# A four-layer graph network on one core: layer 3's seams rearranged (four propagations first, logits inside the late attentions, the check behind the next step's first logits, end flags earlier)

## The chip, the core and the metric

The kernel runs on one core of a Trainium2 chip. A core has five engines with queues of their own: TensorE (PE; its weight loads are shown apart as PEld), VectorE (DVE), ScalarE (ACT), GpSimd (POOL) and SyncE (SP), which here issues most DMAs. They wait for each other by semaphores. The metric is the device time in microseconds (us) of one execution. Times inside an execution are counted from its first instruction.

## The reference, cut to what matters

3327 nodes with 256 features pass through four layers, each of the form `x = x + layer(relu(layernorm(x)))` over the same 3327 x 3327 adjacency. Layers 0 to 2 are products with the adjacency (the second keeps at most 700 entries of a row; the kernel counts a row's entries for this). Layer 3 is the one the change is about:

```python
R = (S + I) / rowsum                       # propagation, S = adj
Z = 0; Xf = Xa = X
for n in range(2):                         # two steps
    q = Xa @ W1.T @ W2.T;  k = Xa @ W3.T
    probs = softmax(q @ k.T)
    A = probs kept up to 0.9 of the row's mass, renormalized   # top-p
    Xf = R @ Xf                            # propagation
    Xa = A @ Xa                            # attention
    Z = Z + Xf @ U1[n].T + Xa @ U2[n].T
h = X + Z;  out = layernorm(h) * g + b
```

The second step's keys come from the first step's attention of all nodes, so all of attention 1 must be done before the first logits of step 2.

## The kernel before, in words

Rows are tiled by 128: T = 26 tiles (the last has 127 rows). All of layer 3 is in `layer_3_in`. PE's order there is written out by hand (`tc.manual_schedule(engines=PE_ALONE)`); the other engines' queues are put in order by the framework from dependencies, program order and priorities, and are then fixed. For one tile m there are these pieces:

- **Propagation** (`propagated_steps`, L1058): 26 blocks, 52 PE instructions, on two adjacency slabs of 832 KB loaded by SP (L1055, three buffers); POOL adds the identity to one block (L1057). The generator yields after each block, and a plan `at = {block: [things to do]}` puts other PE work after a block. Then `PropagationOfFirstStep`: ACT scales the result (`xf`, L1099), SP loads `hT` (L1101); later `turn` (two transposes, L136) and `sums` (8 products, L1111, copied by ACT at L1113).
- **Logits** (`logits_steps`, L912): four chunks into PSUM (two buffers, `ps_row`, shared with node, values and sums), each turned into exponentials by ACT (L931) in a tile `e` (three buffers). `spread` puts two chunks after each of two blocks of a propagation.
- **Search** (`search_steps`): finds for each row the least kept probability. First a threshold from the row's sum (L947 on DVE, L948 to L952 in turns with ACT), then two passes over `e` on ACT (L963, the shortfall; L965, a sign count), then DVE alone: L967 to L1006, among them a 3328-wide pass (L973), maxima (L986, L991), and the masking of `e` (L1002). L1006 ends the search. In the tile loop the two ACT passes and the rest are placed by `passes` after groups 0, 2 and 3 of an attention.
- **Attention** (`Rows.begin`: transposes of the first 8 blocks of the masked `e`, L177, copied by ACT to `eT`, L180; `Rows.finish`: 52 products, L188, with the other transposes between, a yield after each group of four blocks). It needs its own search done. After it `AttentionOfFirstStep`: ACT scales (`xa`, L1069), then `turn`, `node` (key and query of the second step, L241) and `values` (L1082; ACT copies `vs`, L1088, DVE adds `z`, L1089, SP stores it, L1090).

The order before, in the first step: propagations 0, 1, 2 (logits of tiles 0 and 1 inside them), logits 2, then for m = 0 to 25 attention m; up to m = 19 propagation m+3 follows, with the logits of tile m+3, and the turn, node and values of m and `begin(m+1)` put inside (after blocks 0 and 12, and 3, 9, 18, 20). For m = 20 to 25 there is no propagation: logits, turn, node, values and the next transposes simply follow one another. Propagation m's turn and sums stand after groups 1 and 5 of attention m. The search of tile m+2 runs beside attention m.

After attention 25: `failed` (L1024 to L1042, with a matmul that adds up flags over rows, L1034), propagation 23, then `if_failed`: each engine loads a flag into a register and jumps over the repair code (L1241, L1242 in the profile). Behind it the second step begins: key sum and centring of the keys (L887 to L901), logits 0, search 0, propagations 24 and 25 with logits 1 and 2. In the second step every tile has an attention and a propagation, then `finish3`: DVE adds (L1124), normalizes (L1126 to L1131), POOL does three further operations (L1132 to L1134), SP stores to `out` (L1136). At the very end: flags and check of the second step, then a maximum over the row counts (L1416 to L1422) and a second check (L1424) that would run everything again.

Of the kernel before, what the change touches and what calls it, by code (L numbers as in the profile page):

```python
# [45 lines left out]
def kernel(  # L46
# [782 lines left out]
    def layer_3(again, h3, kT0, ksum0, left):  # L829
        tag = "b" if again else "a"  # L830

        only_exp_and_ln()
        with ExitStack() as lctx:
            big, ep, w3, sm3 = (
                lctx.enter_context(tc.tile_pool(name=f"{n}{tag}", bufs=b))
                for n, b in (("big", 1), ("ep", 3), ("w3", 2), ("sm3", 4))
            )
            layer_3_in(tag, big, ep, w3, sm3, h3, kT0, ksum0, left)

    def layer_3_in(tag, big, ep, w3, sm3, h3, kT0, ksum0, left):  # L840
# [53 lines left out]
        def centre(kT, pk, name):  # L894

            mean = sm3.tile([P, 1], F32, tag="kmean", name=f"kmean_{name}{tag}")
            with tc.high_priority():
                nc.vector.tensor_scalar(mean, pk[:, :1], -1.0 / N, None, ALU.mult)
                for r, n in ((0, LOW * P), (DA, N - LOW * P)):
                    k = kT[r : r + DA, :n]  # L900
                    nc.vector.tensor_scalar(k, k, mean[r : r + DA, :], None, ALU.add)  # L901

# [19 lines left out]
        def scores(step, m, kT):  # L922
# [5 lines left out]
            nc.gpsimd.memset(parts[:, len(CHUNKS) :], -1.0)  # L928

            def evict(c, dst, src):  # L930
                nc.scalar.activation(dst, src, AF.Exp, accum_out=parts[:, c : c + 1])  # L931

            return e, parts, logits_steps(kT, qT[:, m * P : (m + 1) * P], e, name, evict)

        def search_steps(step, m, e, parts, st, dens):
# [29 lines left out]
            nc.scalar.activation(junk_a, e, AF.Sign, scale=-1.0, bias=t, accum_out=sign)  # L965
            yield 2
            nc.vector.tensor_scalar(u, sign, 0.5, NP / 2 - AIM, ALU.mult, ALU.add)  # L967
# [147 lines left out]
        def finish3(m, y, acc, name):  # L1115
# [16 lines left out]
            nc.gpsimd.tensor_tensor(z, z, gs, ALU.mult)  # L1132
            nc.gpsimd.tensor_tensor(z, z, bs, ALU.add)
            nc.gpsimd.tensor_tensor(z, z, x3, ALU.add)  # L1134
# [30 lines left out]
        def redone(step, m, kT, name, evict):  # L1165
            e = ep.tile([P, NP], F32, tag="e", name=f"e_{name}")
# [25 lines left out]
        def by_least(step, m, kT, gen, st):  # L1192
# [8 lines left out]
            e = redone(step, m, kT, name, lambda c, dst, src: nc.scalar.activation(dst, src, AF.Exp))  # L1201
# [16 lines left out]
        def general(step, m, kT, gen):  # L1218
# [3 lines left out]
            e = redone(step, m, kT, name, lambda c, dst, src: nc.scalar.copy(dst, src))  # L1222
# [14 lines left out]
        def if_failed(step, flags, st, kT, then):  # L1237
            def inside(level, i, gen):
# [3 lines left out]
                with tc.If(n > 0):  # L1242
                    if level:
                        with tc.tile_pool(name=f"gen{step}", bufs=1) if not gen else nullcontext(gen) as g:
                            for k in range(3):
                                inside(level - 1, 3 * i + k, g)
                    else:
                        e, den, bad = by_least(step, i, kT, gen, st)
                        then(i, e, den, f"t{i}")
                        n_bad = nc.values_load(bad)  # L1250
                        with tc.If(n_bad > 0):
                            then(i, *general(step, i, kT, gen), f"g{i}")
# [5 lines left out]
        EARLY = 3  # L1258
        LATE = 3

        with tc.manual_schedule(engines=PE_ALONE):
# [7 lines left out]
            def find(step, m, st):  # L1269
                return search_steps(step, m, *made[m][:2], st, dens)  # L1270
# [46 lines left out]

            for i in range(EARLY):
                if i == 0:
# [3 lines left out]
                elif i == 1:  # L1323
                    steps = prepare(0, 0, kT0)
                    propagate_first(1, merged({3: [lambda: centre(kT0, mean0(), "0")]}, spread(steps, 9, 19)))
                    run(find(0, 0, st0))
                else:
                    first, second = prepare(0, i - 1, kT0), None
                    propagate_first(i, spread(first))
                    finder = find(0, i - 1, st0)  # L1330
                    run(finder)
            run(prepare(0, EARLY - 1, kT0))
            finder = find(0, EARLY - 1, st0)
            rows = Rows(0, h3)
            rows.begin(0)
            for m in range(T):
                plan = passes(finder)
                if props:
                    p = props.pop(0)
                    plan = merged(plan, {1: [p.turn], 5: [p.sums]})  # L1340
                a = AttentionOfFirstStep(m, rows.finish(m, plan), dens.pop(m), f"{m}")
                after = {3: [a.turn], 9: [a.node], 18: [a.values], 20: [lambda: rows.begin(m + 1)]}
                steps = prepare(0, m + AHEAD, kT0) if m + AHEAD < T else iter(())
                if m + EARLY < T - LATE:
# [127 lines left out]
```

## Time and profile before

| | us |
|---|---|
| median of 3 runs | 2678.3 (2676.7 to 2678.89) |
| profiled execution | 2678.22 |
| its span, first to last instruction | 2676.3 |
| PE busy in the span | 2581.7 |
| first propagation of layer 3 | 957.4 |
| first attention (first step) | 1025.8 |
| attention 19, 20 | 1672.4, 1706.4 |
| attention 24, 25 | 1802.8, 1821.3 |
| end of propagation 23 | 1850.1 |
| first attention (second step) | 1908.9 |
| last product of PE | 2658.9 |

A line of the timeline or of a group reads: start and busy time, engine, line of the kernel, operation, what it writes and reads, how often; in brackets the idle time of the engine before it and what ended it. A window's row gives the stretch, its length, then the busy time and the number of instructions of each engine, the granted PE clock (1.00 is full), the DMA share and GB/s.

### The profile page before, as it was taken

To read this page: it belongs to the slowest core of one execution; us is meant where nothing else is said; L and a number is where in the kernel's file an instruction comes from. 1 tells how busy PE (TensorE), PEld (TensorE's weight loads), DVE (VectorE), ACT (ScalarE), POOL (GpSimd) and SP (SyncE) were. 2 spreads that over 40 slices of the span, in tenths; PEclk is the share of its full clock that TensorE was granted. 3 is DMA by queue.
4 is the path that set the end of the run, shared out by engine and by line. 5 is a ranking of instruction groups with operands and counts; after the bars stand their busy time and mean duration, and the time that the engine had idled before them with its cause. 6 is when DMAs were issued, how large, how long until landed. Compare 5 with 4: busy or idle time off the path is not lost. (4 is left out here: it accounts for less than half of the span.)

```text
span 2676.3 us, 42731 instructions
## 1 busy us (share of the span) xinstructions
PE 2581.7 (96%) x15979; PEld 2219.4 (83%) x15979; DVE 2038.3 (76%) x5488; ACT 1035.3 (39%) x1877; POOL 219.1 (8%) x438
## 2 busy tenths in 40 slices
PE   6999999999999997999999999988999999999997
PEld 6999999999999975777777777766787888788786
DVE  6667788888877748777777776692988888888882
ACT  2110034433011135444444455563454455445441
POOL 2000010000000000000000000000011111111111
PEclk9999999999999998999999999999999999999999
DMA  6555555555666621111111111101122122112211
GB/s 220 145 158 167 168 152 175 172 172 164 187 197 200 190 94 56 60 56 55 54 56 57 58 60 61 50 12 49 62 84 69 64 89 69 64 66 87 69 64 52
DMA packets 141357, 273.42 MB, mean 102 GB/s; under 512 B 15427, under 2 KB 67904, under 8 KB 141120
## 3 DMA queue, kind: packets, MB, share of 16 engines
q1 hardware_dynamic: 115648, 252.49, 29.6%
q10 hardware_dynamic: 25472, 17.92, 2.2%
q8 instruction: 131, 2.15, 0.3%
q14 instruction: 106, 0.87, 0.1%
HBM read 248.20 MB, written 20.45 MB: 100 GB/s over the span
## 5 line engine op out<-in xcount | busy, mean ns | idle before, releaser
L188 PE MATMUL a<-h3a,eT_a 128*128 128x256 f32 x1352 | 325.7, 382 | 8.7 <-ACT eT_a L180 8.5
L1058 PE MATMUL f<-h3a,slab3a 128*128 128x256 f32 x1352 | 323.6, 383 | 0.2 <-issue 0.2
L188 PE MATMUL a<-vs,eT_a 128*128 128x256 f32 x1352 | 322.5, 383 | 0.4 <-ACT eT_a L180 0.2
L1058 PE MATMUL f<-fsa,slab3a 128*128 128x256 f32 x1352 | 312.5, 382 | 0.0
L1058 PEld LDWEIGHTS f<-h3a,slab3a 128*128 128x128 f32 x1352 | 247.7, 190 | 60.4 <-issue 28.1
L1058 PEld LDWEIGHTS f<-fsa,slab3a 128*128 128x128 f32 x1352 | 249.8, 189 | 52.8 <-issue 16.7
L986 DVE MAX8 cand_a<-w 128x8 f32<-128x128 f32 x1352 | 283.3, 280 | 6.7
L188 PEld LDWEIGHTS a<-h3a,eT_a 128*128 128x128 f32 x1352 | 246.1, 190 | 45.0 <-ACT eT_a L180 15.7
L188 PEld LDWEIGHTS a<-vs,eT_a 128*128 128x128 f32 x1352 | 246.3, 190 | 37.5 <-ACT eT_a L180 6.3
L180 ACT COPY eT_a<-pt_a 128x512 f32<-128x512 f32 (+1 forms) x364 | 195.7, 553 | 205.4 <-PE pt_a L177 201.9
L519 PE MATMUL acc_a<-tsa,s_a 128*128 128x128 f32 (+1 forms) x2028 | 268.4, 275 | 0.7 <-DVE tsa L331 0.7
L931 ACT ACTIVATE e_a<-pl_a 128x1024 f32<-128x1024 f32 x208 | 177.9, 860 | 205.8 <-PE pl_a L912 205.7
L519 PE MATMUL acc_a<-tsa,a_a 128*128 128x128 f32 x2028 | 251.2, 275 | 1.8 <-DVE tsa L334 1.8
L519 PE MATMUL acc_a<-rhs,a_a 128*128 128x128 f32 (+1 forms) x2028 | 250.5, 276 | 0.0
L519 PEld LDWEIGHTS acc_a<-tsa,s_a 128*128 128x128 f32 x2028 | 247.4, 192 | 1.2 <-DVE tsa L331 1.0
L519 PEld LDWEIGHTS acc_a<-tsa,a_a 128*128 128x128 f32 x2028 | 239.7, 192 | 3.1 <-DVE tsa L334 2.2
L519 PEld LDWEIGHTS acc_a<-rhs,a_a 128*128 128x128 f32 x2028 | 238.4, 192 | 1.9 <-ACT rhs L411 0.4
L982 DVE SCALAR_TENSOR_TENSOR w<-e_a,t_a 128x896 f32<-128x896 f32 x208 | 225.0, 1082 | 5.2
L177 PE MATMUL pt_a<-ident,e_a 128*128 128x128 f32 x1352 | 200.5, 274 | 13.2 <-DVE e_a L1002 10.9
L177 PEld LDWEIGHTS pt_a<-ident,e_a 128*128 128x128 f32 x1352 | 165.9, 141 | 54.2 <-ACT eT_a L180 11.5
L967 DVE TENSOR_SCALAR u_a<-sign_a 128x1 f32<-128x1 f32 x52 | 8.0, 154 | 245.8 <-ACT junk_a L965 245.8
L973 DVE SCALAR_TENSOR_TENSOR w<-e_a,t_a 128x3328 uint8<-128x3328 f32 x52 | 191.6, 3684 | 3.6
(202 smaller groups left out, 3498.6 us busy)
## 6 DMA issues: line engine op xcount, KB each, us to landing
slab3a<-in_adj_t_dram SPq DMA_DIRECT2D x104, 832.0 KB, 5.9
a_a<-in_adj_t_dram SPq DMA_DIRECT2D x312, 256.0 KB, 3.3
a_a<-in_adj_t_dram SPq DMA_DIRECT2D x156, 320.0 KB, 3.4
x_dram<-x_a ACTq DMA_DIRECT2D x39, 256.0 KB, 2.7
x_a<-x_dram SPq DMA_DIRECT2D x26, 256.0 KB, 3.1
hT_dram<-xT_a ACTq DMA_DIRECT2D x26, 128.0 KB, 3.7
hT<-hT_dram SPq DMA_DIRECT2D x26, 128.0 KB, 2.0
z_dram<-z SPq DMA_DIRECT2D x26, 128.0 KB, 1.7
```

The source lines that it names most:

```text
L177: nc.tensor.transpose(pt[:, j, :], e[:, k * P : (k + 1) * P], ident)
L180: last_turned.append(nc.scalar.copy(eT[:, : len(blocks), :], pt[:, : len(blocks), :]))
L188: nc.tensor.matmul(acc[:, :width], ready[g][:, j, :], rhs[:, k, :], start=(k == 0), stop=(k == T - 1))
L519: nc.tensor.matmul(self.acc[:, g, at : at + wide], quads[n][:, k - CUTS[c][0], :], t, start=(k == 0 and n in (1, 4)), stop=(k == H - 1 and ...
L931: nc.scalar.activation(dst, src, AF.Exp, accum_out=parts[:, c : c + 1])
L967: nc.vector.tensor_scalar(u, sign, 0.5, NP / 2 - AIM, ALU.mult, ALU.add)
L973: nc.vector.scalar_tensor_tensor(junk, e, t, e, ALU.is_lt, ALU.mult, accum_out=got)
L982: nc.vector.scalar_tensor_tensor(w[:, : (b - a) * P], eg, t, eg, ALU.is_lt, ALU.mult, accum_out=below[:, g : g + 1])
L986: nc.vector.max(cand[:, 8 * k : 8 * k + 8], w[:, (k - a) * P : (k - a + 1) * P])
L1058: nc.tensor.matmul(acc[:, :D], slab[g][:, j, :], xf[:, k, :], start=(n == 0), stop=(n == T - 1))
```

## The change

Four propagations instead of three stand first; the first three's turn and sums go inside the following propagations, the fourth's comes after it. From m = 1 on, attention m carries the turn and sums of propagation m+3. For the first tile of each step the sign pass is done on DVE (`alone`) instead of ACT. Attentions without a propagation behind them (m = 19 to 23) carry the logits of tile m+3 after groups 4 and 6; the next tile's transposes follow at once, then the turn, and node and values go after groups 0 and 2 of the next attention. Propagation 23 stands between attentions 24 and 25. Propagation 24 follows attention 25 and carries its turn, node and values, the flags, the key sum, the centring and the logits of the second step's first tile. Only then comes the check. Behind it: search 0, propagation 25 with the logits of tiles 1 and 2. At the end the flags of the second step are computed inside the last propagation, the last tile's three POOL operations go to DVE, and the maximum over the counts with its flag is computed after layer 2, its register loaded before the check of the second step. The repair code (`by_least`, `general`, `redo_first`) gets a scratch tile and redoes the first logits and a key's centring; it is jumped over in these runs.

```diff
+        def exp_of_logits(step, m, kT, e, parts, name=""):
...
             nc.scalar.activation(junk_a, e, AF.Relu, scale=-1.0, bias=t, accum_out=short)
             yield 1
-            nc.scalar.activation(junk_a, e, AF.Sign, scale=-1.0, bias=t, accum_out=sign)
+            if alone:
+                nc.vector.tensor_scalar(junk, e, t, None, ALU.is_lt, ALU.add, accum_out=sign)
+            else:
+                nc.scalar.activation(junk_a, e, AF.Sign, scale=-1.0, bias=t, accum_out=sign)
             yield 2
...
-            nc.gpsimd.tensor_tensor(z, z, gs, ALU.mult)
-            nc.gpsimd.tensor_tensor(z, z, bs, ALU.add)
-            nc.gpsimd.tensor_tensor(z, z, x3, ALU.add)
+            engine = nc.vector if m == T - 1 else nc.gpsimd
+            engine.tensor_tensor(z, z, gs, ALU.mult)
+            engine.tensor_tensor(z, z, bs, ALU.add)
+            engine.tensor_tensor(z, z, x3, ALU.add)
...
-        EARLY = 3
+        EARLY = 4
...
+                return search_steps(step, m, *made[m][:2], st, dens, m == 0)
...
             for i in range(EARLY):
+                plan = {}
+                if props:
+                    p = props.pop(0)
+                    plan = {5: [p.turn], 16: [p.sums]}
...
-                    first, second = prepare(0, i - 1, kT0), None
-                    propagate_first(i, spread(first))
+                    propagate_first(i, merged(spread(prepare(0, i - 1, kT0)), plan))
                     finder = find(0, i - 1, st0)
-                    run(finder)
-            run(prepare(0, EARLY - 1, kT0))
-            finder = find(0, EARLY - 1, st0)
+                    if i + 1 < EARLY:
+                        run(finder)
+            p = props.pop(0)
+            p.turn()
+            p.sums()
             rows = Rows(0, h3)
             rows.begin(0)
+            left_over = {}
             for m in range(T):
-                plan = passes(finder)
+                plan = merged(passes(finder), left_over)
                 if props:
                     p = props.pop(0)
                     plan = merged(plan, {1: [p.turn], 5: [p.sums]})
+                interleaved = m + EARLY < T - LATE
...
+                    plan = merged(plan, {4: [begin_logits], 6: [lambda: next(steps)]})
                 a = AttentionOfFirstStep(m, rows.finish(m, plan), dens.pop(m), f"{m}")
...
-                else:
-                    run(steps)
-                    for k in sorted(after):
-                        after[k][0]()
+                elif m + 2 < T:
+                    rows.begin(m + 1)
+                    a.turn()
+                    left_over = {0: [a.node], 2: [a.values]}
+                elif m + 1 < T:
+                    left_over = {}
+                    after = {1: [a.turn], 4: [a.node], 8: [a.values], 22: [lambda: rows.begin(m + 1)]}
+                    propagate_first(T - LATE, after)
                 finder = find(0, m + AHEAD, st0) if m + AHEAD < T else None
-            flags0 = failed("0", st0)
-            propagate_first(T - LATE, {})
...
+            steps = prepare(1, 0, kT1)
+            propagate_first(T - LATE + 1, {
+                1: [a.turn], 3: [first_flags], 4: [a.node], 8: [a.values, sum_second],
+                11: [centre_second], 17: [lambda: next(steps)], 22: [lambda: next(steps)],
+            })
+            first_e, first_parts = made[0][:2]
...
-        if_failed(0, flags0, st0, kT0, redo_first)
+        if_failed(0, flags0, st0, kT0, redo_first, lambda name: first_e, redo_second_steps_first)
...
-            centre(kT1, key_sum(kT1, ksum1, "1")(), "1")
             st1 = new_state("1")
-            run(prepare(1, 0, kT1))
             run(find(1, 0, st1))
...
+            p = props.pop(0)
+            plan = {2: [p.turn], 10: [p.sums]}
+            propagate_first(
+                T - 1, merged(spread(prepare(1, 1, kT1), 0, 6), spread(prepare(1, 2, kT1), 14, 20), plan)
+            )
+            run(find(1, 1, st1))
+            finder = find(1, 2, st1)
...
+                if m == T - 1:
+                    plan = {4: [lambda: flags1.extend(failed("1", st1))]}
                 finish3(m, y, propagate_second(m, plan), f"{m}")
                 finder = find(1, m + AHEAD, st1) if m + AHEAD < T else None
-            flags1 = failed("1", st1)
...
+        at_end()
...
             lctx.close()
-        layer_3(again, h3, kT0, ksum0, left)
+            if not again:
+
+                nc.vector.tensor_reduce(most, counts, AX.X, ALU.max)
+                pm = one_bank("pm")
+                nc.tensor.transpose(pm[:1, :P], most, ident)
+                nc.vector.tensor_reduce(most1, pm[:1, :P], AX.X, ALU.max)
+                nc.vector.tensor_copy(flag, most1)
+        layer_3(again, h3, kT0, ksum0, left, at_end)
...
+    all_layers(False, lambda: loaded.append(nc.values_load(flag[0:1, 0:1])))
```

## The prediction

> **What bounds the kernel now.** I read the page first (engine shares, slices), then TensorE's waits, then windows around layer 3's seams, then VectorE's timeline there.
>
> ```profile
> PE 2581.7 (96%) x15979; PEld 2219.4 (83%) x15979; DVE 2038.3 (76%) x5488; ACT 1035.3 (39%) x1877; POOL 219.1 (8%) x438
> ```
>
> TensorE (PE) sets the pace. In the steady first step of layer 3 a tile takes 33.96 us with PE busy 33.71; in the second step PE is busy 288.94 of 289. Nothing is to be won there. The time lies in the seams. Windows (PE busy, PEld, DVE, ACT, POOL, granted clock):
>
> ```profile
> 1289.70:1323.66 33.96, 33.71 (x168) 26.50 (x166) 23.88 (x73) 16.93 (x32) 0.66 (x3) 1.00 0.17 59
> ...
> 1729.55:1755.43 25.88, 22.99 (x116) 16.72 (x115) 23.93 (x73) 16.57 (x31) 0.20 (x2) 1.00 0.04 12
> ```
> ```profile
> 1010.63:1024.04 13.41, 2.50 (x9) 1.18 (x9) 13.41 (x36) 3.22 (x9) 0.27 (x3) 0.50 0.00 0
> 1024.04:1028.31 4.27, 4.27 (x14) 3.60 (x15) 4.27 (x21) 1.38 (x3) 0.00 (x0) 0.50 0.00 0
> 1850.08:1857.41 7.33, 0.56 (x3) 0.53 (x3) 1.59 (x4) 0.47 (x1) 0.45 (x1) 0.79 0.75 273
> ```
>
> Seam 1 (before the first attention): PE stands while VectorE (DVE) finishes search 0, then runs at clock 0.50. Late tiles (20 to 22, no propagation beside them): 25.88 us each, PE stalling behind ScalarE (ACT), but DVE is busy 23.93. Seam 2 (the check): 7.33 us nearly empty. DVE in the late tiles:
>
> ```profile
> 1717.32 0.15 DVE L967 TENSOR_SCALAR u_a<-sign_a 128x1 f32<-128x1 f32 x1 [9.23 <-ACT junk_a L965]
> ...
> 1741.99 0.16 DVE L1006 RECIPROCAL den_a<-all_kept 128x1 f32<-128x1 f32 x1
> 1743.20 0.15 DVE L967 TENSOR_SCALAR u_a<-sign_a 128x1 f32<-128x1 f32 x1 [1.04 <-ACT junk_a L965]
> ```
>
> PE's waits from 1700 to 1909:
>
> ```profile
> PE a L188 <- ACT eT_a L180: 5.7, 7, 1.6
> PE pk_mean_1a L887 <- DVE ktotal_1a L891: 5.3, 1, 5.3
> PE pl_a L912 <- ACT e_a L931: 3.8, 4, 2.7
> PE pkq L241 <- ACT xT_a L138: 3.6, 6, 0.7
> ```
>
> The four add up to 18.4 us and none names DVE's search: the late tiles wait for ACT's copies. But search 22 starts after 9.23 us of DVE idleness; from there to the end of search 25 (1819.4) DVE rests only about 1 us per search. A search takes 24.8 us (1743.20 to 1768.04) with a z addition inside. So the late tiles have a second limit close behind the first.
>
> **Unit costs** (start-to-start in the timeline): propagation 52 x 0.2165 = 11.26; attention products the same; its later 18 transposes 1.95, the first 8 0.87; logits 1.91 + 1.35 = 3.26; node 0.5; values 1.72; turn 0.22; a propagation's turn and sums 1.95.
>
> **Seam 1.** Moved in: propagation 3 (11.26) and three more turn-and-sums ahead of attention 0, while sums 0 also goes forward: 11.26 + 4 x 1.95 = 19.1 us of PE work over a hole of about 17 us plus 2.1 us lost at half clock. Forward from 972.5, where propagation 1 starts: propagation 1 with its sums 16.6, to 989.1; 2: 16.5, to 1005.6; 3: 16.5, to 1022.1; its own turn and sums with two ACT waits (0.6 and 0.7) 4.0, to 1026.1; first transposes and a copy 1.1: attention 0 starts at 1027.2. Is search 0 ready? Its logits end 1.95 later; its sign pass moves to DVE beside ACT's other pass. That form (3328 elements, scalar operation with a sum) is not in the trace: from below 2 us (the centring at L901 takes 1.09 for 1664), from above 3.69 (L973). I take 3.7, the accumulating row; ACT's 3.07 + 0.19 runs beside it anyway, so between the ends lies 0.4 us. Then L967 comes at about 993.8 and, with 29.6 us as now (search 1 is interleaved), ends at 1023.4, just ahead of PE. Attention 1 starts 32.0 later (33.96 less 1.95, since no sums are left for tile 0): 1059.2, before 1061.1. **-1.9.** One propagation more is then done. The moved slab loads (two of 832 KB, 5.9 us to landing) go through SP with three buffers as now: the second slab is needed 5.2 us + logits + turn after the first, so it is hidden; uncovered it would cost about 3. The propagation's hT load (2.0) no longer waits for a third tile's buffer; POOL's identity addition (0.49) rides along. Search 1's passes still end before attention 1 needs it (1040 against 1055). Steady tiles: the same work, 0 (bounds -0.05 to +0.05 each, 18 tiles).
>
> **Late attentions.** Attention 19 now starts at 1670.5 (before 1672.4) with no propagation after it. Its logits, then node and values of the tile before, go inside: PE needs 11.26 + 1.95 + 3.26 + 2.22 + 0.87 + 0.22 = 19.8 per tile instead of 25.9, so DVE binds. The node's qT copy (ACT's DMA queue) and the z store (SP) move along with node and values; nobody waits for them before the next step. Search 21 ends at 1706.2 (1708.1 less 1.9); search 22 no longer finds its sign missing, and three searches at 24.95 end search 24 at 1781.1, before 1793.9. Attention 24 starts 1.3 later, 1782.4. PE alone: 15.4 + 0.5, then propagation 23 with turn, node, values and the next transposes 14.6, then attention 25 with sums 23 15.2: 1828.1. Search 25 is ready in time (1806 against 1811). Two charges. In-order queues (the logits' PSUM buffers come free by DVE's z addition, which sits in DVE's queue among searches; eT copies sit behind ACT work that waits for DVE): 0 to 6, I take 2, near the 1.59 us wait such a copy shows now. Clock: PE now stands 6 to 8 us before attention 24. Here a rule speaks against the change. The Trainium skill (TensorE: Matmul & The Clock Gate, What's actually happening) says that an idle window of about 3.4 us halves PE's clock until a busy window of about 3.4 us has passed; by that a gap costs 1.7, and a shorter one nothing. The rows are harder: 4.27 us at 0.50 after the restart, 2.1 lost, and at 1873.55 a 2.74 us gap already brought a window at 0.58. I take 2.5. Attention 25 ends at 1832.6.
>
> **The check.** Propagation 24 with turn, flags, node, values, key sum, centring and logits of the next step: 11.26 + 0.22 + 0.24 + 0.5 + 1.72 + 0.28 + 3.26 + 0.3 = 17.8, to 1850.4: about where propagation 23 ends now (1850.08). DVE, SP and POOL branch earlier, under it; slabs for 25 wait for SP's jump, but that lies 8 us earlier. ACT still has to evacuate this propagation first, then jumps:
>
> ```profile
> 1850.12 0.47 ACT L1099 ACTIVATE xf<-f,rinv 128x256 f32<-128x256 f32 x1 [8.38 <-PE f L1058]
> ```
> ```profile
> DVE ktotal_1a L891 <- ACTq L1242: 15.2, 1, 15.2
> ```
>
> DVE resumes at 1855.01, so ACT's jump costs 4.8. The skill (Advanced Engine Details and Errata, Control Flow Timing) puts a compare-and-branch at about 0.11 us; by it, L967 would come 4.7 sooner. I take the row. Behind ACT's jump wait search (1,0) and every logit copy of propagation 25. 0.3 + 4.8 + 1.5 (threshold) + 3.3 (short beside sign) + 0.3 = 10.2: L967 at 1860.6, before 1872.5. Search 0 takes 29.6 as now: 1890.2. PE meanwhile: jump gap 0.9, propagation 25 with the logits of two tiles and two pairs of turn and sums 11.26 + 6.52 + 3.9 + 1.3 (ACT waits) = 23.0, stalls behind ACT 5: near 1879. So the search decides; attention 0 at 1890.2 + 1.4 + 2.5 (cold clock) = 1894.1, before 1908.86. **-14.8 in all up to here.**
>
> **The end.** The last tile's three additions go from POOL (2.40, L1132 to L1134) to DVE, 3 x 0.46 = 1.4; flag matmul 0.24 goes ahead: -0.75. SP's wait is the output store's: 127 packets of 1 KB follow one another, landing 7.2 after issue (2671.05), and both jumps come after. That stays; only the second flag's load, 0.4, leaves SP's path. **-1.1.** The count reduction at 2666.16 to 2667.26 lies beside that store: removing it gives 0. Its PE transpose and DVE steps now stand ahead of propagation 0: between 0 and 0.8 (0.37 + DVE 0.6 before L540), I take **+0.3**.
>
> Sum -15.6. Profiled execution 2678.22 (span 2676.3 + 1.9): 2662.6; the median of the runs is 2678.3, so I predict 2662.6.
>
> **Rivals.**
> - *Better*: search (1,0) is not interleaved (24.8, -4.8), no clock loss (-5.0), no queue loss (-2.0): 2650.8. For it: DVE's order is made anew. Against: both first searches are stretched to 29.6 now. 0.20.
> - *Smaller*: PE stalls behind ACT's passes in propagations 2 and 3 (now 1.01 and 4.98, so +4) and queue losses of 6 (+4): 2670.6. 0.20.
> - *Nothing*: the late tiles gain only search 22's 9.2 and the end 1.1; clock (5.0) and queue losses (3) take it back and the check hides nothing more: about 2676. 0.05.
> - *Slower*: the threshold sums of the next tile (L947, L951) land in DVE's queue behind the whole running search. Then each of searches 22 to 25 waits for 1.5 + 6.6 us of ACT before L967, 33 instead of 24.95: search 25 ends at 1838.6, attention 25 starts at 1840, ends 1855 instead of 1832.6: 2685. It decides from 3.9 us per late search on. Against: at 1730.34 L947 sits inside search 22 today. 0.04.
>
> **How the numbers follow.** Main case 0.51: 2657 to 2668 by the bounds of queue loss and clock. Better 0.20, smaller 0.20, nothing 0.05, slower 0.04. A measurement tells 0.2% (5.4 us) from no change. Faster 0.91, within 0.05, slower 0.04. The range 2649 to 2672 leaves out the last two and the tails.
>
> **What would show it.** No PE gap and clock 1.00 from 990 to 1040; attention 0 near 1027. L967 intervals of about 25 us in the late tiles without sign waits; PE waiting for L1002 there. L967 of step two about 10 us after propagation 24. I am wrong if DVE waits for signs there, if L967 intervals exceed 28, if PE waits for slabs in propagations 3 or 25, or if ACT's jump is short.

## The result and the profile after

The changed kernel takes 2659.2 us (median of four runs, 2657.1 to 2660.2) against 2677.5 us for the kernel before on the same chip (2676.5 to 2678.9): a ratio of 0.993, 95% interval 0.9913 to 0.9948. Predicted were 2662.6 us, with a range of 2649 to 2672. The profiled execution took 2657.14 us with a span of 2655.3.

The page of the changed kernel, busy time by engine:

```profile
PE 2575.5 (97%) x15979; PEld 2215.1 (83%) x15979; DVE 2050.0 (77%) x5495; ACT 1030.1 (39%) x1873; POOL 222.6 (8%) x435
```

No instruction of weight has gone; what has gone is idle time. To find where, one mark per seam is enough. The starts of the first product of an attention, counted from the first product of propagation 0 (957.36 in the profile before, 954.36 after, since layers 0 to 2 differ by some us from profile to profile):

| first product of | before | after | change |
|---|---|---|---|
| attention 1, step one | 103.75 | 104.87 | +1.1 |
| attention 19 | 715.04 | 716.09 | +1.1 |
| attention 24 | 845.43 | 827.65 | -17.8 |
| attention 0, step two | 951.51 | 933.35 | -18.2 |
| attention 2, step two | 1010.23 | 993.10 | -17.1 |
| attention 25, step two | 1676.79 | 1659.75 | -17.0 |
| last instruction | 1718.98 | 1700.90 | -18.1 |

Nearly the whole gain arises between attentions 19 and 24. Seam 1 loses 1.1 us (with one propagation more done in it), the check's seam gives 0.4, attentions 0 to 2 of step two lose 1.1, the end gives 1.0.

**Late tiles.** VectorE's timeline of the changed kernel (start, duration, operation; a wait would stand in brackets). In the profile before, one of these rows carried a wait of 9.23 us for the sign:

```profile
1730.42 0.15 DVE L1016 RECIPROCAL den_a<-all_kept 128x1 f32<-128x1 f32 x1
1730.49 0.14 DVE L977 TENSOR_SCALAR u_a<-sign_a 128x1 f32<-128x1 f32 x1
...
1755.05 0.15 DVE L1016 RECIPROCAL den_a<-all_kept 128x1 f32<-128x1 f32 x1
1755.12 0.14 DVE L977 TENSOR_SCALAR u_a<-sign_a 128x1 f32<-128x1 f32 x1
```

Each search (L977, which was L967) begins in the moment in which the search before it ends (L1016), 24.6 us apart: VectorE binds. The windows (in the columns of the prediction's windows) show a late tile and the check, one after the other:

```profile
1737.50:1762.18 24.68, 20.75 (x106) 15.03 (x105) 23.80 (x74) 15.92 (x30) 0.20 (x2) 1.00 0.02 7
1844.80:1850.13 5.33, 0.03 (x2) 0.01 (x1) 0.02 (x1) 0.47 (x1) 0.05 (x1) 0.95 0.88 321
```

In the late tile TensorE rests 3.9 of 24.7 us, but at clock 1.00: its pauses are short ones for ScalarE's transposed copies, not one long one for the search. From 1660 to 1845 this row heads its waits, and no row names the end of a search (L1012):

```profile
PE a L188 <- ACT eT_a L180: 9.4, 8, 2.6
```

At the check all engines are all but idle for 5.3 us (ScalarE works 0.47) while the DMA engines are 88% busy. TensorE's waits around it, from 1845 to 1890:

```profile
PE pl_a L913 <- ACT fsa L1123: 7.1, 1, 7.1
PE f L1068 <- ACTq L1253: 5.3, 1, 5.3
```

L1253 is the check's branch: TensorE waits for ScalarE's queue to get past it. The longer wait, in propagation 25, is for a copy of 0.35 us.

### The profile page after: what moved, and what is told of

It is laid out like the page before. It is cut to its first block, busy times and chain, and to the rows that moved or that the text cites. A ratio compares the mean times of both kernels' runs of the same rounds, so it can differ in the third digit from the quotient of the medians.

```text
span 2655.3 us, 42726 instructions
## 1 busy us (share of the span) xinstructions
PE 2575.5 (97%) x15979; PEld 2215.1 (83%) x15979; DVE 2050.0 (77%) x5495; ACT 1030.1 (39%) x1873; POOL 222.6 (8%) x435
## 5 line engine op out<-in xcount | busy, mean ns | idle before, releaser
L1012 DVE SCALAR_TENSOR_TENSOR e_a<-e_a,all_least 128x3328 f32<-128x3328 f32 x52 | 192.1, 3695 | 1.2
```

The source lines that it names most:

```text
L1012: nc.vector.scalar_tensor_tensor(e, e, least, e, ALU.is_ge, ALU.mult, accum_out=st["kept"][:, m : m + 1])
```

## The experiments

Each is the changed kernel with one edit. A total is known to some 4 us here (the interval of a ratio is about 0.0015 to each side), so smaller effects are read from the marks of the table above, which repeat to some 0.1 us between seams. One thing has to be taken off: four of the profiles (the check as before, the end as before, search 1 behind the logits, the store in two) have 1.1 to 1.4 us of half clock in seam 1 that the changed kernel's does not have (attention 0 at 74.2 to 74.5 instead of 73.07; the last section says more).

### Undoing one part at a time

**Seam 1 as before**: three propagations early, the loop ahead of the first attention and the sign of its tile 0 as they were.

```
-        EARLY = 4
+        EARLY = 3
```

> The changed kernel with seam 1 as before: three propagations ahead of the first attention, no turn and sums there, sign of tile 0 on ScalarE; everything else as changed. Theory L (the late tiles made the gain, and the fourth early propagation is what takes the propagation away from attention 19): attention 19 has a propagation beside it again, 33.96 us instead of some 23, and seam 1 gets 1.1 us shorter by the measured start of attention 1: +10, about 2669. Rival S (the early propagation is paid in full in seam 1, nothing is won by it): -1 to 0, about 2658 to 2659.

Measured: 2673.2 us, ratio 0.9986 (0.9978 to 0.9995), +15.0 against the changed kernel's ratio (0.0056 x 2677), more than expected. Attention 1 starts at 103.04 (1.8 sooner), but attentions 19 to 24 take 128.2 us instead of 111.6. VectorE's timeline of this kernel shows why:

```profile
1679.66 0.15 DVE L977 TENSOR_SCALAR u_a<-sign_a 128x1 f32<-128x1 f32 x1 [9.24 <-ACT junk_a L972]
1713.62 0.15 DVE L977 TENSOR_SCALAR u_a<-sign_a 128x1 f32<-128x1 f32 x1 [9.24 <-ACT junk_a L972]
1739.12 0.15 DVE L977 TENSOR_SCALAR u_a<-sign_a 128x1 f32<-128x1 f32 x1 [1.00 <-ACT junk_a L972]
1766.11 0.15 DVE L977 TENSOR_SCALAR u_a<-sign_a 128x1 f32<-128x1 f32 x1 [2.27 <-ACT junk_a L972]
```

With a propagation beside attention 19 one more search interval lasts 34 us with 9.24 us of idle VectorE in it. The propagation that the change does early is paid in seam 1 with only 1.8 us, and ends the 34 us rhythm one tile sooner. Why it is more than expected: of the 16.7 us, 9.7 are that interval (33.96 instead of 24.22), 3.0 are two further late signs (the last two rows), and 3.9 are attention 24, which begins 6.1 us after its search instead of 2.2. By the marks the end comes 14.7 later. Theory L stands, rival S falls.

**Late tiles in the order of before.** What had been put inside the attentions follows them again.

```
-                    plan = merged(plan, {4: [begin_logits], 6: [lambda: next(steps)]})
...
-                    rows.begin(m + 1)
-                    a.turn()
-                    left_over = {0: [a.node], 2: [a.values]}
+                    if m + AHEAD < T:
+                        run(prepare(0, m + AHEAD, kT0))
+                    a.turn()
+                    a.node()
+                    a.values()
+                    rows.begin(m + 1)
```

> The changed kernel with the late tiles' work in the order of before: the next logits, the turn, node and values after each attention, then the first transposes of the next. Theory L (interleaving lets TensorE work under ScalarE's copies, so that VectorE's searches bind at 24.9 us): four tiles at 25.9 us, and a search that finds its sign missing for about 9 us once: from attention 19 to attention 24 some 121 us instead of 111.6, +10, about 2669. Rival D (the searches bind either way, the order of TensorE's work is hidden under them): 24.9 a tile, no more than +3, about 2660 to 2662.

Measured: 2666.4 us, ratio 0.9966 (0.9953 to 0.998): +9.6 by the ratios, +6.4 by the marks; attention 24 starts at 835.88 instead of 827.65. The size is that of theory L, its reason is not: VectorE's searches keep their rhythm (in the table's count they start at 752.5, 777.1, 801.8 and 827.5, in the changed kernel at 751.3, 776.1, 800.8 and 825.4). TensorE's timeline of this kernel around attentions 23 and 24:

```profile
1783.50 2.86 PE L188 MATMUL a<-h3a,eT_a 128*128 128x256 f32 x12
1786.92 0.44 PE L136 MATMUL pt_a<-ident,xa 128*128 128x128 f32 x2 [0.56 <-ACT xa L1079]
1787.82 0.71 PE L241 MATMUL pkq<-xT_a,kq 128*128 128x128 f32 x4 [0.46 <-ACT xT_a L138]
1788.37 1.88 PE L1092 MATMUL u<-u2s,xT_a 128*128 128x512 f32 x4
1790.09 1.04 PE L177 MATMUL pt_a<-ident,e_a 128*128 128x128 f32 x8
1791.36 2.00 PE L188 MATMUL a<-h3a,eT_a 128*128 128x256 f32 x8 [0.24 <-ACT eT_a L180]
```

Search 24 had ended at 1782.0, but attention 24 begins 9.3 us later: TensorE is behind with attention 23 and its turn, node and values. In the changed kernel the same distance is 2.2 us. So there are two chains of nearly the same length, TensorE's serial one and VectorE's; the interleaving shortens the first until only the second counts.

**The check as before**: propagation 23 no longer between attentions 24 and 25, and from the flags to the last propagation the code of before.

```
-                    propagate_first(T - LATE, after)
...
+            flags0 = failed("0", st0)
+            propagate_first(T - LATE, {})
...
+            centre(kT1, key_sum(kT1, ksum1, "1")(), "1")
...
+            run(prepare(1, 0, kT1))
+            run(find(1, 0, st1))
```

> The changed kernel with the seam between the two steps as before: no propagation between attentions 24 and 25, propagation 23 after attention 25, then the check, and only then key sum, centring and the next logits. Theory C (propagation 23 fills TensorE's wait for search 25, which now ends about 1804.6, and the key sum and logits under propagation 24 hide about 5 us of what followed the jump): attention 25 starts behind the search near 1806 and ends near 1820, propagation 23 ends near 1834.5, from there to step two's first attention 58.8 as before: 1893.3 instead of 1887.7, +5.6, about 2665. Rival N (from attention 24 to the second step's first attention the two kernels take 106.1 and 105.7, so this part is worth nothing): 0 to +1, about 2660. If ScalarE's copies rather than the search hold step two's first attention, as the 7.06 us wait for the copy of the sums says, then this version, where they lie elsewhere, may even end below +5.

Measured: 2663.3 us, ratio 0.9954 (0.9938 to 0.9969): +6.4 by the ratios, +6.7 by the marks, of which 1.1 are the half clock in seam 1, so 5.6 for the part. TensorE's waits of this kernel from 1770 to 1900:

```profile
PE pt_a L177 <- DVE e_a L1012: 6.8, 1, 6.8
PE pk_mean_1a L887 <- DVE ktotal_1a L891: 5.6, 1, 5.6
```

Both rows are those of theory C: attention 25 waits 6.8 us for search 25, because no propagation stands between, and the key mean waits behind the jump. Rival N compared 106.1 with 105.7 and concluded that the part is worth nothing; that was wrong, since before the change search 25 was in time only because the late tiles were slow. Up to step two's attention 0 the new check gains 6.8 us; 1.0 of it is lost again in attentions 0 to 2, which follow each other after 29.4 and 29.3 us here and after 29.5 and 30.25 in the changed kernel.

**The end as before**, with the flags of step two after the last tile again.

```
-            engine = nc.vector if m == T - 1 else nc.gpsimd
+            engine = nc.gpsimd
...
-                    plan = {4: [lambda: flags1.extend(failed("1", st1))]}
```

> The changed kernel with the end as before: the last tile's three products and sums on GpSimd, and the flags of the second step after the last tile (the count reduction stays at the front). By the sum of the prediction: 0.75 and 0.4 come back, +1.1, about 2660.3. If SP's load of the second flag never left the path, as its start 0.4 us after the first join says: +0.75. Rival: the store's landing alone sets the end and the additions were hidden: 0.

Measured: 2657.9 us, ratio 0.9936 (0.9922 to 0.9949), no difference that the totals can show. By the marks the stretch from step two's last attention to the end lasts 42.1 instead of 41.15: +0.9, between the two sums. In nine of the other kernels, whose end is the changed one's, this stretch lasts 41.13 to 41.21, so the rival's 0 is excluded.

The three main parts are worth 15.0, 9.6 and 6.4 us by the ratios when each is taken away alone, 31 together (by the marks 14.7, 6.4 and 5.6, 27 together), against a gain of 18: they are not additive. Each takes away what would be late next.

### Trying the waits that are left

**ScalarE begins search 1 of step two only behind tile 2's logits.**

```
+            with tc.issue_after(evicted[-1].ins):
                 run(find(1, 1, st1))
```

> The changed kernel, where ScalarE begins search 1 of the second step only behind the last logit copy of tile 2. Theory A (in propagation 25 TensorE stood 7.06 us because a copy of 0.35 us lay in ScalarE's in-order queue behind search 1's start, which waits for a sum that VectorE makes late): the wait goes, TensorE is ready near 1880, search 0 ended at 1880.0, attention 0 of step two starts near 1881.5 instead of 1887.7: -6, about 2653. Rival R (search 1 then comes late, and attention 1 of step two waits for it): search 1 loses some 10 us of start but is needed only 23 us after attention 0: 0 if it does run late, between -6 and 0.

Measured: 2665.3 us, ratio 0.9956 (0.9941 to 0.9971), +7 where -6 was expected (by the marks +6.6, with 1.4 of half clock in seam 1: +5.2). The 7.06 us wait is gone, but TensorE's waits of this kernel have a new head among the seams:

```profile
PE pt_f L136 <- ACT xf L1109: 15.9, 3, 12.4
```

The copy of propagation 25 now lies behind search 1's start, which still waits for VectorE's sum. Same queue, another victim, and a later one. Search 1 comes late too: attention 2 follows attention 1 after 31.7 us instead of 30.3.

**ScalarE's passes of search 1 of step one behind the copy of propagation 2.**

```
+                        with tc.issue_after(props[-1].evicted.ins):
                             run(finder)
```

> The changed kernel, where the passes of search 1 of the first step (and of search 0) lie in ScalarE's queue behind the copy of the propagation just ended. Theory A (TensorE's wait of 2.94 us in propagation 3 is for that copy, which queued behind two passes of 3.07): attention 0 of step one starts near 1024.5 instead of 1027.4: -2.9, about 2656.3. Rival S (search 1 then comes late for attention 1 or steals ScalarE from tile 2's logits): 0 or worse.

Measured: 2662.8 us, ratio 0.9941 (0.9925 to 0.9956): +2.9 by the ratios, within the totals' uncertainty. The profiled execution is the slowest of this kernel; by its marks the end comes 6.2 us later, all of it in the first seam: attention 0 of step one starts at 79.27 instead of 73.07. TensorE's timeline of this kernel:

```profile
1010.09 2.32 PE L1068 MATMUL f<-h3a,slab3a 128*128 128x256 f32 x10
1015.84 2.08 PE L913 MATMUL pl_a<-kT_0a,qT 64*128 64x512 f32 x4 [3.43 <-ACT e_a L934]
1020.17 0.80 PE L913 MATMUL pl_a<-kT_0a,qT 64*128 64x128 f32 x4 [2.25 <-ACT e_a L934]
1020.90 5.20 PE L1068 MATMUL f<-h3a,slab3a 128*128 128x256 f32 x12
```

The wait of 2.94 us is gone; behind it the passes come later and stand in front of tile 2's logit copies, 5.7 us in two waits, and the gap halves the clock (12 products take 5.20 us, where at full clock they take 2.86).

**VectorE reads propagation 24, so that ScalarE reaches the check sooner.**

```
+                  if m == T - 2:
+                    nc.vector.tensor_scalar(self.xf, acc[:, :D], rinv[:, m : m + 1], None, ALU.mult)
-                11: [centre_second], 17: [lambda: next(steps)], 22: [lambda: next(steps)],
+                11: [centre_second], 13: [lambda: next(steps)], 16: [lambda: next(steps)],
```

> The changed kernel, where VectorE instead of ScalarE evacuates propagation 24, and tile 0's logits of the second step stand at steps 13 and 16 of it instead of 17 and 22, so that ScalarE's last work ahead of its jump ends some 4 us sooner. Theory J (all engines wait at the check for the last one's jump, and ScalarE's, 4.8 us, is the last): TensorE's wait of 5.3 us at the check falls to what VectorE's own jump takes behind propagation 24, unknown between 1 and 4.8; search 0 of step two starts as much sooner; but TensorE's 7.06 us wait follows search 0's start, so all of it moves: -1 to -4, middle -2.5, about 2656.7. Rival P (the wait is TensorE's own jump, or VectorE's is as long as ScalarE's): 0.

Measured: 2660.1 us, ratio 0.9936 (0.9921 to 0.9951), no gain. TensorE's waits of this kernel:

```profile
PE f L1068 <- DMA slab3a<-in_adj_t_dram: 9.3, 1, 9.3
...
PE pl_a L913 <- ACT fsa L1126: 3.6, 1, 3.6
```

And SP's own, from 1835 to 1870:

```profile
SPq L1065 <- DVEq L1256: 12.0, 1, 12.0
```

The wait for ScalarE's jump has become one of 9.3 us for propagation 25's slabs. SP, which has long jumped, waits 12 us with its first slab load until VectorE's counter moves, and VectorE jumps only after the new read. SP's queue, which the prediction had followed only to its own jump, hangs on VectorE's as well. The other wait shrank by 3.4 us, so that step two's attention 0 (934.40) came only 1.05 later.

**The last store in two.**

```
-                nc.sync.dma_start(out[m * P : m * P + n, :], z[:n, :])
+            for a, b in [(0, P)] if m < T - 1 else [(0, 112), (112, LAST)]:
+                nc.sync.dma_start(out[m * P + a : m * P + b, :], z[a:b, :])
```

> The changed kernel, where the last store of 127 rows is issued as 112 and 15 rows. Theory Q (127 packets of 1 KB ran one after another on one DMA engine, 7.2 us from issue to landing, where 128 rows took 1.7): 112 rows land in about 2, 15 rows behind one another in about 1 to 2, and one issue more on SP: landing about 3 to 3.5 after the first issue, -4, about 2655. Rival F (the 7.2 us are the fixed cost of the last store's completion): 0, or +0.1 for the second issue.

Measured: 2656.7 us, ratio 0.9927 (0.9913 to 0.994), within the totals' uncertainty. From step two's last attention to the end it is 39.1 instead of 41.15: -2.0. The trace's packet records show the mechanism. In the changed kernel the 127 rows are packets of 1 KB one behind the other, from 2643.80 to 2649.83, some 0.047 us each, and the store lands 6.84 us after its issue. As 112 and 15 rows the packets run beside one another: 14 of the 15 are over at 2646.66, and the last one begins at 2647.51, when a packet of 16 KB of instructions ends; so the 15 rows land 3.5 us after their issue, not in 1 to 2. Nor would a faster landing have helped much: SP's own first jump (2646.10 to 2649.42) ends 0.9 us after the landing at 2648.56, while in the changed kernel it was over at 2647.53 and SP waited for the store until 2650.19. The jump is now the limit.

**VectorE makes search 1's sum sooner** (the head of that search at higher priority, its rest behind the end of search 0).

```
+            with tc.high_priority() if m == 1 else nullcontext():
                 nc.vector.tensor_reduce(total, parts, AX.X, ALU.add)
                 ...
```

> The changed kernel, where in both seams VectorE makes search 1's sum and threshold about 3 us sooner, in the second quarter of search 0 instead of the third (higher priority for the head of that search), and the rest of search 1 stays behind the end of search 0. Theory O (TensorE's waits of 2.94 in propagation 3 and 7.06 in propagation 25 are ScalarE's in-order queue: a short copy behind two passes behind a sum that VectorE makes in the middle of search 0): each falls by the 3 us that the sum comes sooner: propagation 3 waits 0, propagation 25 some 4; with the half clock that sometimes follows the 2.94 us gap gone too: -5 to -7, about 2653. Rival Q (the copies wait for TensorE's or the passes' own length, wherever the sum stands): 0, 2659.

Measured: 2658.7 us, ratio 0.9939 (0.9925 to 0.9952): nothing that the totals show, and by the marks a loss of 2.1 (attention 0 of step one at 73.95, +0.9; the end at 1702.96). In the first seam the sum came 2.1 us sooner and the 2.94 us wait went, and TensorE's waits from 994 to 1028 now read:

```profile
PE pt_f L136 <- ACT xf L1109: 2.2, 1, 2.2
PE pl_a L913 <- ACT fsa L1123: 0.6, 1, 0.6
```

They are the same sort of wait one propagation later, behind the head of search 2, which in turn waits for its sum (6.6 us on ScalarE). The gap of 2.2 us also halved the clock: the next four products take 1.80 us instead of 1.03. In the second seam the edit did not move the sum (13.0 us after search 0's start, 13.1 without it), so there it says nothing.

**ScalarE reads propagation 24 only behind the check**, and tile 0's logits stand at steps 13 and 16.

```
-                props.append(PropagationOfFirstStep(m, acc))
+                if m == T - 2:
+                    unread.append(acc)
+                else:
+                    props.append(PropagationOfFirstStep(m, acc))
...
             st1 = new_state("1")
+            p = PropagationOfFirstStep(T - 2, unread.pop())
             run(find(1, 0, st1))
```

> The changed kernel, where ScalarE reads propagation 24's sums only behind the check (the same instruction, later), and tile 0's logits stand at steps 13 and 16 of that propagation, so that ScalarE reaches the check some 1.3 us ahead of TensorE's end and VectorE as early as now. Theory J (the 5.3 us are ScalarE's jump, which lasted 5.2 us beside two slab loads and 2.5 us without them, and TensorE's own jump of 3.7 lies under its last products): TensorE goes on 2 to 3.6 us sooner, search 0 of step two starts 3 sooner, and the wait in propagation 25 moves along: -2 to -3.5, about 2656.5. Rival K (code is fetched beside the slab loads whichever way, and the last jump stays at 5 us from its start): -1.3 or less.

Measured: 2656.1 us, ratio 0.9925 (0.991 to 0.994). By the marks step two's attention 0 starts at 930.05, 3.3 us sooner, and the end comes 3.3 us sooner: theory J. TensorE's waits of this kernel from 1840 to 1895:

```profile
PE pl_a L913 <- ACT fsa L1123: 9.4, 1, 9.4
PE u L1121 <- ACT xT_f L138: 1.0, 1, 1.0
PE f L1068 <- PEq L1253: 1.0, 1, 1.0
```

What is left at the check is TensorE's own jump, 1.0 us. TensorE then waits longer in propagation 25 (9.4 for 7.1): search 0 begins 3.4 us sooner, but TensorE, without the half clock that followed the gap, is at the wait 5.7 us sooner.

**Sign of the first searches on ScalarE.**

```
-                return search_steps(step, m, *made[m][:2], st, dens, m == 0)
+                return search_steps(step, m, *made[m][:2], st, dens, False)
```

> The changed kernel with the sign pass of both first searches on ScalarE again. Theory O (both seams hang on search 0's progress, since search 1's sum lies inside it in VectorE's order): search 0 starts about 2.8 us later (3.26 + 3.26 on ScalarE instead of 3.7 beside 3.26), and so do search 1's passes and TensorE's waits in both seams: +3 to +5.5, about 2663. Rival Z (TensorE binds in both seams and has room before the searches): 0 to +0.5.

Measured: 2659.9 us, ratio 0.9939 (0.9924 to 0.9955). Search 0 of step one does start 2.9 us later (39.1 instead of 36.3 in the table's count), yet attention 1 comes at 105.93 and step two's attention 0 at 933.99: rival Z. VectorE's order came out otherwise in the build, with search 1's sum nearer to search 0's start, so the waits of TensorE in sum stayed as they were. Moving the sign to VectorE brought nothing that the totals can show; by the marks the end comes 1.7 us later without it (0.6 up to step two's attention 0, 1.05 more up to attention 2, which follows attention 1 after 31.3 us instead of 30.25). Since VectorE's order changed too, this is not the sign's worth alone. Theory O, that all hangs on search 0's start, is too simple.

**Three edits together** (sum sooner, read behind the check, store in two).

> Three edits together: search 1's sum sooner in both seams, propagation 24's sums read behind the check, and the last store in two. If the gains add: -5 -2.5 -2 = -9.5, about 2650. If the second seam becomes bound by search 0 (it ended 7.7 us before attention 0 there, so there is room for the first two): the same. Rival: the waits only change places: 2656 or more.

Measured: 2653.8 us, ratio 0.9914 (0.9901 to 0.9928), the fastest of all. By the marks it ends at 1697.05, 3.9 us ahead of the changed kernel: 2.1 of them at the end of the kernel, 2.2 up to step two's attention 0, less 0.4 between. Alone, the second and the third edit had brought 3.3 and 2.0. Some 1.4 of that is missing here: the sum made sooner costs 0.9 in the first seam (attention 0 of step one at 73.96), as when it was alone, and some tenths in step two.

## Where the prediction was right and wrong

**Seam 1: -1.9 predicted, +1.1 measured.** The filled hole and the full clock came as forecast. The miss of 3.0 us is nearly all one wait that the sum has at nothing: in its step "3: 16.5, to 1022.1" propagation 2's turn stands inside propagation 3, and that turn needs propagation 2's copy. ScalarE's timeline of the changed kernel:

```profile
1002.70 0.20 ACT L952 ACTIVATE mean_a<-total_a 128x1 f32<-128x1 f32 x1 [6.40 <-DVE total_a L951]
...
1004.28 3.07 ACT L967 ACTIVATE junk_a<-e_a,t_a 128x3328 uint8<-128x3328 f32 x1
...
1007.47 3.07 ACT L972 ACTIVATE junk_a<-e_a,t_a 128x3328 uint8<-128x3328 f32 x1
...
1010.54 0.45 ACT L1109 ACTIVATE xf<-f,rinv 128x256 f32<-128x256 f32 x1
```

The copy of 0.45 us queues behind two passes, which queue behind a sum. TensorE waits 2.94 us. (The turn of propagation 3, for which the sum took a wait of 0.6, waited 0.83.) The rival "Smaller" had this (+4), so it was seen and valued at too little. The forecast of search 0 being 29.6 us long, interleaved, was wrong as well (24.8), without consequence, because TensorE binds there. The sign pass on VectorE took 3.68, the upper bound that was taken.

**Late attentions: 111.9 us from attention 19 to 24 predicted, 111.6 measured.** The mechanism (searches at 24.9 without a missing sign) and the size hold. Of the charges "I take 2" and "I take 2.5" for queues and clock neither came: TensorE did not stand 6 to 8 us in front of attention 24, because waits for ScalarE's copies spread its slack over the tile. So the sign "PE waiting for L1002 there" was wrong, and from attention 24 to the end of attention 25 it took 45.0 instead of 50.2.

**The check: right in sum by luck, wrong inside.** From the end of attention 25 to step two's attention 0, 61.5 was predicted and 60.7 measured. Propagation 24 took the forecast 17.8. From its end two paths run to attention 0, and both sums were off. The search began 10.6 us after it (10.2 forecast) but took 24.6 us and not 29.6 (the rival "Better" had this), so it ended 4.6 us ahead of the forecast. TensorE's path to the first transposes was summed to 28.9 us and measured 41.6 (1844.82 to 1886.43). The "jump gap 0.9" measured 5.3: TensorE's own jump was priced, and not that the first instruction behind it waits for ScalarE's (4.4 more). The waits for ScalarE were 8.6 where 6.3 had been taken, 7.06 of them for one copy behind search 1's passes (2.3 more). And the half clock had been charged behind the search, not on this path, where it came after both gaps, for 6.8 us each (4.8 more); about 1 us is left over. So "So the search decides" fell: TensorE decided, at a time that happened to lie 0.8 from the forecast.

**The end: -1.1 predicted, -1.0 by the marks.** But the second flag's load still comes after the first jump's join, so that 0.4 us did not leave the path. And "both jumps come after" misread the profile before: SP's first jump (2664.87 to 2667.46) lay under the store, which landed at 2671.05; only the second came after. The cost of the earlier count reduction (+0.3) cannot be told from the scatter of layers 0 to 2.

**Not foreseen:** step two's attentions 0 to 2 follow each other after 29.5 and 30.25 us instead of 29.4 and 29.3, since searches 1 and 2 now begin later relative to attention 0: 1.1 us lost. With the check as before they follow each other after 29.4 and 29.3 again.

**In sum** the parts missed by +3.0 (seam 1), -0.3 (late attentions), -5.2 (attentions 24 and 25), -0.8 (the check) and +1.1 (attentions 0 to 2). That 2662.6 and 2659.2 lie so close is in part the offsetting of these misses. The mechanism of the late tiles, which carries the gain, was right.

Still open is the wait in propagation 25. It changed its place when search 1 began later, grew to 9.4 us with a sooner check and fell to 3.6 us when TensorE came later itself, but no run here made an order of ScalarE's and VectorE's queues in which attention 0 begins as soon as search 0 ends, 6 us sooner.

## What to carry to other kernels

A stage in which two chains have nearly the same length gives back little for shortening one; undo the parts one at a time and expect that their worths do not add. Work that fills a hole early is worth what it takes away late: here a propagation that costs 1.8 us in a hole ended a 34 us rhythm one tile sooner. When an engine waits for a tiny copy, ask what stands in front of that copy in its in-order queue and what that waits for; rearranging the queue handed the wait to another instruction in three tries here (search 1 behind the logits, its passes behind a copy, its sum sooner). Taking a copy out of the way of the jump gained 3.3 us.

## What the runs showed of the hardware

**A jump is slower beside loads.** In the changed kernel ScalarE's way over the check lasts 5.2 us (1844.87 to 1850.06 in the trace), with two slab loads of 832 KB issued at 1844.42 and 1844.92. Where ScalarE reads behind the check, it lasts 2.5 us (1844.98 to 1847.50): an older load lands at 1846.6, and no slab load is issued until 1848.61. So it is in every profile: 4.5 to 5.2 us in the eleven in which ScalarE reads a propagation just ahead of the check, 2.5 to 2.7 in the three in which it need not, and 2.4 to 2.7 at the second step's check, where no slabs are loaded. GpSimd's falls from 5.6 to 2.9. The share of busy DMA engines from 1844 to 1851 in 40 slices, of the changed kernel, where the jump lies wholly in the loads:

```profile
DMA  0000000299994299899979989999899989888974
```

and of the kernel that reads behind the check:

```profile
DMA  7788998984210000040000010100000985497998
```

The packet records say where the time goes. With free DMA engines the first packet of 8 KB of instructions begins 0.6 to 1.2 us after ScalarE's branch (0.94 in the kernel where VectorE reads, 0.92 at the changed kernel's second check); beside the slab loads it begins 2.9 to 3.7 us after it (3.61 in the changed kernel). In both cases ScalarE goes on 1.5 to 1.7 us after that packet began (2.1 once). So the code waits for the DMA engines behind the slabs. No edit moved the loads alone, so this rests on the records and not on an experiment.

The Trainium skill (Advanced Engine Details and Errata, Control Flow Timing), which the prediction weighed, gives a compare-and-branch about 0.11 us. The branch's own record on ScalarE lasts 0.05 us here; what costs 2.5 to 5.2 us is the way to the next instruction.

**A gap of 2 to 4 us may or may not halve the clock.** Eight profiles have the same gap, 2.94 or 2.95 us, ahead of propagation 3's turn. In four of them the next ten products take 2.32 or 2.33 us, in the other four 3.5 to 4.0, and attention 0 then starts at 74.2 to 74.5 instead of 73.1 to 73.2. The changed kernel's, and that of the kernel with the end as before:

```profile
1011.05 0.44 PE L136 MATMUL pt_f<-ident,xf 128*128 128x128 f32 x2 [2.94 <-ACT xf L1109]
1011.32 2.32 PE L1068 MATMUL f<-h3a,slab3a 128*128 128x256 f32 x10
```
```profile
1009.89 0.69 PE L136 MATMUL pt_f<-ident,xf 128*128 128x128 f32 x2 [2.95 <-ACT xf L1109]
1010.37 3.56 PE L1068 MATMUL f<-h3a,slab3a 128*128 128x256 f32 x10
```

So 1.1 to 1.4 us of the scatter between otherwise equal stretches comes from one gap. Its length does not decide: a gap of 2.18 us (sum sooner) halved the clock, one of 3.77 us (sign on ScalarE) did not. The 3.4 us that the prediction weighed is thus no threshold for a gap. What does fit is where the gap falls. In each profile's clock record the stretches at half clock begin whole multiples of 3.413 us after one another, and apart from the one at the kernel's end they last 3.41 us or a multiple. Laid on this grid (TensorE's ends are modelled), from 900 to 2630 us every stretch at full clock in which TensorE was busy 1.42 us or less is followed by one at 0.50, and every one with 1.45 or more by one at 1.00. The gap of 2.94 us lies across two stretches in the changed kernel (busy 1.64 in the first, and 1.00 after it) and within one where the store is in two (busy 1.09, and 0.50 after it). In layers 0 to 2 the two kinds mix between 1.45 and 1.69.

**A store of 127 rows is slow.** Its 127 packets of 1 KB go one behind the other and it lands some 7 us after its issue; as 112 and 15 rows the packets go beside one another, and the second part, issued 0.4 us after the first, lands after 3.5, one of its packets held up by a packet of instructions.
